# A gated recurrence on one core: one transpose of 128 columns in place of two of 64, and another division of the input products over the steps

## The chip, the cores and the metric

The kernel runs on one core of one Trainium2 chip. The core has a matrix engine (TensorE, PE in the profile; its weight loads are the row PEld), a vector engine (VectorE, DVE), a scalar engine (ScalarE, ACT), a general engine (GpSimd, POOL) and a queue that issues most of the DMAs (SyncE, SP). TensorE writes its results into PSUM, from where VectorE and ScalarE read them; all other data is in SBUF. The metric is the device time of one execution in microseconds (us), and a smaller one is better.

## The reference

The input `x` has 8 sequences of 512 steps with 512 features, and `cond_1024` is the first state `h`, 8 by 512. The result is `x` plus the states of this recurrence:

```
fused = sigmoid(concat([x_t, h]) @ w_W + w_b)
r, z = split(fused)
m = x_t @ wx_W + wx_b + r * (h @ wh_W + wh_b)
h = z * h + (1 - z) * tanh(m)
```

All is in float32. The 512 steps depend on each other through `h`. The products with `x_t` don't.

## The kernel before

**Layout.** The 512 units of the state are cut into four quarters of 128 (index `k` as input, `c` as output) with 32 units of each quarter in each quarter of the partitions. Two output quarters are called half A, the other two half B. The state of each half and step is a tile `hTA` or `hTB`, in eight buffers (L150). The batch is only 8, so one matrix multiplication holds four steps' columns as 32 stationary columns, of which a step uses eight rows of the result. The four parts `j` of the result (32 rows each) are computed by four matrix multiplications side by side on the array (L388). A float32 multiplication is recorded as two MATMUL rows, so that one `k` of a product is eight MATMUL rows, in two groups of four that run together.

**One step.** The steps run in the order of the program (L366); each engine takes its instructions in the order in which they are written. TensorE's order is the constant `ORDER` (L27): bank A (256 columns for the two `k` of hTA, then 192 for the two of hTB), bank D (128 columns for each of the four `k`), bank H (64 columns, two `k`), and then one portion of products with `x` for later steps, which the generator `products` (L296) hands out up to its next `yield` (L393). Bank A holds the three raw values of half A (h, z and r, 64 columns each) and 64 columns that half B needs; bank D holds half B's z and r; bank H the rest of half B's h. There are two sets of banks, one for four steps, then the other.

After the matrix work VectorE and ScalarE make the next state. For half A: `turn_r(0)`, `turn_h(0)`, `turn_z(0)` (L470 to L472), each a VectorE transpose of 64 columns out of bank A; ScalarE takes the sigmoid of r into `md0A` and of minus z into `hd0A`; two scans `memory(0, 0)` and `memory(0, 1)` on VectorE (L462) form the argument of tanh; ScalarE writes tanh into the state tile (L463). For half B: `turn_part` (L452) out of bank A, `turn_r(1)` (L477) out of bank D, `turn_h(1)` (L479) out of bank H, `turn_z(1)` (L480) out of bank D. Between them stand the two scans `update(0, 0)` and `update(0, 1)` (L465) that make the next hTA. Then come `memory(1, 0)`, `memory(1, 1)`, the tanh of half B, and `update(1, 0)`, `update(1, 1)`, that make the next hTB. The next step's bank A needs hTA for its first two `k` and hTB for its last two. `update(0, 1)` is made to wait for half B's sigmoid of r (`r_done`, L481), and `memory(1, 0)`, that reads its result, comes behind it. The tiny memsets of the tile `idle` (L441 behind `turn_z(0)`, and two at the end of each step, L570) are places for waits and delays: L441 waits for the transpose of `turn_h(0)`.

**The input products.** Two groups of four steps share one set of products (six products of half size and a shared one, with sums `sx` made on GpSimd by `x_sum` and weight differences `tw`). They are made during eight steps. Each portion is two groups of four parts per set of columns, from a generator with eight `yield`s: 384 columns in each of four steps, then 288, 96 and 192, 192 and 96, and 288, which is 288 in each of four. The first portion falls on the step with i mod 8 = 4. The generator runs for 62 sets, steps 4 to 499; steps 500 to 511 have no product. The sums and copies that the products need are made at the end of certain steps (L507 to L561); among them `x_sum(o + 2, 2)` at u = 3, where u is i mod 8.

Of the kernel before, what the change touches and what calls it, by code (L numbers as in the profile page):

```python
# [7 lines left out]
F32 = mybir.dt.float32  # L8
BF16 = mybir.dt.bfloat16
AF = mybir.ActivationFunctionType  # L10
# [3 lines left out]
P = 128  # L14
# [3 lines left out]
HU = 64  # L18
# [1 line left out]


DVE_FILL = 23
IDLE = 3
LAST = 4
SYNC = mybir.DependencyInfo(mybir.DependencyClass.Sync, mybir.DependencyReason.DATA)

# [22 lines left out]
def tile_cond_rnn_residual(  # L49
# [39 lines left out]
    nc = tc.nc  # L89
# [7 lines left out]
    work = ctx.enter_context(tc.tile_pool(name="work", bufs=4))  # L97
# [54 lines left out]
    md0 = [[pair(n, f"md0{n}{i}", 32, m) for i in range(2)] for n, m in (("A", 2), ("B", 3))]  # L152
# [72 lines left out]
    def act(key, out_, in_, func, **kw):  # L225
        inst = nc.scalar.activation(out_, in_, func, **kw).ins  # L226
# [58 lines left out]
    def x_sum(o, n):  # L285

        t_ = [q[o % 2] for q in sx]
        a, b, op = [
            (x_half(o, 1, 0), x_half(o, 1, 1), ALU.add),
            (t_[0], x_half(o, 0, 0), ALU.subtract),  # L290
            (x_half(o, 0, 0), x_half(o, 1, 0), ALU.subtract),
            (x_half(o, 0, 1), t_[1], ALU.subtract),
        ][n]
        nc.gpsimd.tensor_tensor(t_[n], a, b, op)

    def products(o):  # L296

        t_ = [q[o % 2] for q in sx]
        p1 = (0, x_half(o, 0, 0), wx_of(0, 0))
        p2 = (0, x_half(o, 0, 1), wx_of(1, 0))  # L300
        p3 = (0, t_[3], wx_of(1, 1))
        p4 = (1, x_half(o, 1, 1), tw[3])
        p6 = (0, t_[1], tw[1])
        p7 = (1, t_[2], tw[2])

        def pair(left, right, k, c0=0, c1=WIDE):
            for j in range(NQ):
                bank, lhs, rhs = left if j < 2 else right
                mm(
                    xps[bank][32 * j : 32 * j + 32, COLS.start + c0 : COLS.start + c1],  # L310
                    lhs[:, k],
                    rhs[:, k, j % 2, c0:c1],
                    start=right is p7 and k == 0 and j >= 2,
                )
# [10 lines left out]
        pair(p1, p7, 0)  # L325
        yield
        pair(p1, p7, 1)
        yield
        pair(p2, p6, 0)
        yield  # L330
        pair(p2, p6, 1)
        yield
        pair(p4, p3, 0, 0, 288)
        yield
        pair(p4, p3, 0, 288)
        shared(0)
        yield
        shared(1)
        pair(p4, p3, 1, 0, 96)
        yield  # L340
        pair(p4, p3, 1, 96)
        yield

    def take(it, n=None):
        while n is None or n > 0:
# [20 lines left out]
    for i in range(T):  # L366
        g, s = divmod(i, GS)
        c, t = divmod(i, TC)
        ps = banks[g % 2]
# [5 lines left out]
        for n in (ORDER if i else FIRST).split():  # L375
# [3 lines left out]
            bank, k = n[0], int(n[1])  # L379
# [15 lines left out]
        rows = slice(B * s, B * s + B)  # L395

        def scan(c_, out_, d0, d1):
# [6 lines left out]
            ).ins  # L404

        pa = ps["A"][:, HU:] if i else xps[0][:, :HALF]
        raw = {
            "h": (pa[:, :HU], ps["H"]),
            "z": (pa[:, HU : 2 * HU], ps["D"][:, :HU]),
            "r": (pa[:, 2 * HU :], ps["D"][:, HU:]),  # L410
        }

        def turned(n, hf):
            t_ = work.tile([P, 2, 32], F32, tag=f"t{n}{hf}", name=f"t{n}{hf}_{i}")
            inst = nc.vector.transpose(t_.rearrange("p c n -> p (c n)"), raw[n][hf]).ins  # L415
            return t_[:, :, rows], inst

        r_done = [None, None]
        h_done = [None, None]

        def turn_r(hf):
            tr, _ = turned("r", hf)
            r_done[hf] = act(
                ("r", hf, g % 2, s),
                md0[hf][g % 2][:, rows, :, 1 + hf].rearrange("p n c -> p c n"),
                tr,
                AF.Sigmoid,
            )
# [9 lines left out]
        def turn_z(hf):  # L438
            tz, _ = turned("z", hf)
            if hf == 0:  # L440
                inst = nc.vector.memset(idle[:, IDLE - 1 :], 0.0).ins  # L441
                tc.add_manual_dep(inst, h_done[0].name, SYNC)
            act(
                ("zc", hf, i % 2),
                hd0[hf][i % 2][:, :, :, 2].rearrange("p n c -> p c n"),
                tz,
                AF.Sigmoid,
                scale=-1.0,
            )

        def turn_part():
            nc.vector.transpose(md1[1][g % 2][:, :, :, 0].rearrange("p n c -> p c n"), ps["A"][:, :HU])  # L452
# [18 lines left out]
        turn_h(0)  # L471
        turn_z(0)  # L472
        memory(0, 0)
        memory(0, 1)
        if i:
            turn_part()
        turn_r(1)  # L477
        update(0, 0)
        turn_h(1)  # L479
        turn_z(1)  # L480
        tc.add_manual_dep(update(0, 1), r_done[1].name, SYNC)  # L481
        if i == 0:
# [9 lines left out]
        memory(1, 0)  # L492
        memory(1, 1)
        update(1, 0)
        update(1, 1)
# [5 lines left out]
        o, u = divmod(i, 2 * GS)  # L501
        nxt, two = o + 1 < NG // 2, o + 2 < NG // 2
# [15 lines left out]
        if u == 0:  # L518
            spread(2 * o + 1, "D")
            if o and nxt:  # L520
                nc.scalar.copy(xps[0][Q01, lo], step_bias[Q01])
                nc.scalar.copy(xps[1][Q23, lo], step_bias[Q23])
        elif u == 1:
            spread(2 * o + 1, "A")
            if o == 0:
                seed(3)
        elif u == 2:
            if o == 0:
                nc.scalar.copy(xs[0][:, SC], xps[0][:, COLS])
            elif nxt:  # L530
                nc.scalar.copy(both[Q23, HALF:], xps[0][Q01, lo])
                nc.vector.tensor_copy(both[Q23, :HALF], xps[1][Q23, lo])
            if two:
                nc.scalar.copy(xps[0][Q01, COLS], bias[Q01, COLS])
        elif u == 3:
            if o == 0:
                nc.scalar.copy(xs[1][:, SC], xps[1][:, COLS])
            if two:
                x_sum(o + 2, 2)
        elif u == 4 and nxt:  # L540
            if o:
                add_(xs[1][Q01, SC], xps[1][Q01, COLS], u3[Q23], ALU.add)
            spread(2 * o + 2, "A")
            if two:
                x_sum(o + 2, 0)
        elif u == 5 and nxt:
            if o:
                add_(xs[1][Q23, SC], u3[Q23], both[Q23], ALU.add)
            if two:
                nc.scalar.copy(xps[0][Q23, COLS], xps[0][Q01, COLS])  # L550
                x_sum(o + 2, 1)
            spread(2 * o + 2, "D")
        elif u == 6 and nxt:
            spread(2 * o + 2, "H")
            if two:
                nc.vector.memset(xps[1][Q01, COLS], 0.0)
# [12 lines left out]
        for n in range(IDLE - 1):  # L569
# [101 lines left out]
```

## Time and profile before

| | |
|---|---|
| three timed runs | 1681.18, 1681.23, 1681.54 us; median 1681.23 us |
| profiled execution | 1681.52 us, of which 1679.7 us are its span, from the first instruction to the last |
| granted TensorE clock | 1.000 |
| busy in the span | VectorE 1402.8 us, ScalarE 1190.5 us, GpSimd 327.2 us; for TensorE see below |
| DMA | 30.14 MB; the DMA engines are busy under a tenth of the time after the first of 40 slices |

A row of the timeline view has the start in us from the span's start, the time from the first start to the last end, engine, line and operation, what is written and read with shapes, and how many instructions were merged (x16). In brackets stands the idle time of that engine in front of it and what ended it. A row of the groups view has count, busy time in us, mean ns of one, and the idle time of the engine in front of them. A matrix multiplication's row is longer than the time until the next one may start, so spacing is read from start to start. A VectorE row likewise overlaps the next by some 0.05 to 0.10 us, and where the instruction waits, part of the wait can stand within it.

### The profile page before, as it was taken

How to read it: one execution, taken by the hardware profiler on the slowest of the kernel's cores; microseconds unless marked ns; L12 is line 12 of the kernel's file. 1: busy time of each engine (PE TensorE's matmuls, PEld its weight loads, DVE VectorE, ACT ScalarE, POOL GpSimd, SP SyncE). 2: the span in 40 equal slices, each digit the busy share in tenths (PEclk: the TensorE clock that was granted, in tenths of full speed). 3: DMA queues.
4: the chain of work that ended last, by engine and by line, in shares of the span. 5: the costliest groups of instructions: out<-in, count | busy, mean ns of one | idle time of the engine just before them, and what ended most of it. 6: DMA issues, size and time to landing. Idle time of an engine off the chain costs nothing.

```text
span 1679.7 us, 110201 instructions
## 1 busy us (share of the span) xinstructions
PE 1667.8 (99%) x46078; PEld 1237.3 (74%) x46078; DVE 1402.8 (84%) x10213; ACT 1190.5 (71%) x5884; POOL 327.2 (19%) x1290
## 2 busy tenths in 40 slices
PE   8999999999999999999999999999999999999998
PEld 5777777777777777777777777777777777777776
DVE  6888888888888888888888888888888888888886
ACT  4777777777777777777777777777777777777775
POOL 2221121111211211112112121121121211211211
PEclk9999999999999999999999999999999999999999
DMA  4000000000000000000000000000000000000000
GB/s 178 17 4 17 17 17 17 12 9 17 17 17 17 4 17 17 17 17 4 17 17 17 17 16 5 17 17 17 17 4 17 17 17 17 4 17 11 11 11 10
DMA packets 11452, 30.14 MB, mean 18 GB/s; under 512 B 1220, under 2 KB 1732, under 8 KB 10952
## 3 DMA queue, kind: packets, MB, share of 16 engines
q1 hardware_dynamic: 10800, 22.94, 3.9%
q8 instruction: 360, 5.90, 1.5%
q14 instruction: 140, 1.15, 0.2%
q10 hardware_dynamic: 152, 0.16, 0.0%
HBM read 14.70 MB, written 8.39 MB: 14 GB/s over the span
## 4 chain that ended last, share of the span: by engine, by line
PE 97%; DVE 2%; DMA 1%; ACT 0%; issue 0%
PE A L195 48%; PE D L195 26%; PE xp L195 17%; PE H L195 7%; DMA wd<-in_wd_dram 1%; DVE tr L415 0%; DMA rows<-in_bias_dram 0%; DVE m L399 0%; DVE md1B L452 0%; DVE tw L283 0%; DVE tz L415 0%; DVE md1A L431 0%; DVE hTA L399 0%; DVE hTB L399 0%; ACT hTB L226 0%
## 5 line engine op out<-in xcount | busy, mean ns | idle before, releaser
L195 PE MATMUL A<-wa,hTA 128*32 128x256 f32 x8176 | 535.3, 379 | 3.0 <-DVE hTA L399 3.0
L195 PE MATMUL A<-wa,hTB 128*32 128x192 f32 x8176 | 436.2, 331 | 0.0
L195 PEld LDWEIGHTS A<-wa,hTA 128*32 128x32 f32 x8176 | 255.6, 122 | 233.0 <-DVE hTA L399 171.3
L572 POOL TENSOR_TENSOR ot<-xin,hTB 128x16 f32<-128x16 f32 x503 | 124.8, 248 | 1312.0 <-DVE hTB L399 1301.0
L195 PEld LDWEIGHTS A<-wa,hTB 128*32 128x32 f32 x8176 | 250.8, 123 | 165.8 <-DVE hTB L399 145.4
L195 PE MATMUL D<-wd,hTA 128*32 128x128 f32 x8192 | 317.6, 273 | 1.2 <-DMA wd<-in_wd_dram 1.2
L195 PE MATMUL D<-wd,hTB 128*32 128x128 f32 x8192 | 317.5, 273 | 0.0
L226 ACT ACTIVATE md0A<-tr 128x16 f32<-128x16 f32 x512 | 112.8, 220 | 231.0 <-DVE tr L415 221.6
L195 PEld LDWEIGHTS D<-wd,hTA 128*32 128x32 f32 x8192 | 257.2, 122 | 22.2 <-DMA wd<-in_wd_dram 1.5
L195 PE MATMUL xp<-tw,sx 128*32 128x384 f32 x1984 | 265.3, 406 | 0.0
L415 DVE STREAM_TRANSPOSE tr<-A 128x64 f32<-128x64 f32 x511 | 127.9, 250 | 137.0 <-PE A L195 127.7
L195 PEld LDWEIGHTS D<-wd,hTB 128*32 128x32 f32 x8192 | 240.4, 122 | 0.0
L399 DVE TENSOR_TENSOR_SCAN hTB<-hd0B,hTB 128x24 f32<-128x24 f32 x1024 | 159.9, 198 | 94.4 <-ACT hTB L226 94.4
L195 PE MATMUL H<-wa,hTB 128*32 128x64 f32 x8192 | 208.2, 219 | 0.0
L195 PE MATMUL xp<-wx,xin 128*32 128x384 f32 x1056 | 207.9, 486 | 0.0
L399 DVE TENSOR_TENSOR_SCAN hTA<-hd0A,hTA 128x24 f32<-128x24 f32 x1024 | 194.8, 190 | 0.0
L195 PEld LDWEIGHTS H<-wa,hTB 128*32 128x32 f32 x8192 | 185.5, 122 | 0.0
L226 ACT ACTIVATE hTB<-hTB 128x16 f32<-128x16 f32 x512 | 121.3, 237 | 78.4 <-DVE hTB L399 66.2
L226 ACT ACTIVATE hd0B<-tz 128x16 f32<-128x16 f32 x512 | 115.7, 226 | 74.9 <-DVE tz L415 27.6
L226 ACT ACTIVATE hTB<-m 128x8 f32<-128x8 f32 x1024 | 163.8, 208 | 4.4
L226 ACT ACTIVATE hTA<-m 128x8 f32<-128x8 f32 x1024 | 160.5, 206 | 2.2
L399 DVE TENSOR_TENSOR_SCAN m<-md0A,md1A 128x16 f32<-128x16 f32 x1024 | 142.2, 181 | 8.8
(103 smaller groups left out, 2586.2 us busy)
## 6 DMA issues: line engine op xcount, KB each, us to landing
xin<-in_x_dram SPq DMA_DIRECT2D x31, 256.0 KB, 3.5
out_dram<-ot SPq DMA_DIRECT2D x31, 256.0 KB, 2.1
wx<-in_wx_dram SPq DMA_DIRECT2D x4, 768.0 KB, 6.8
wa<-in_wa_dram SPq DMA_DIRECT2D x4, 512.0 KB, 9.6
wd<-in_wd_dram SPq DMA_DIRECT2D x1, 768.0 KB
wd<-in_wd_dram SPq DMA_DIRECT2D x1, 256.0 KB, 11.2
out_dram<-ot SPq DMA_DIRECT2D x1, 192.0 KB, 1.9
head<-in_xh_dram ACTq DMA_DIRECT2D x1, 144.0 KB, 4.8
```

What stands on the lines that cost most here:

```text
L195: nc.tensor.matmul(out_, lhsT, rhs, start=start, stop=False, skip_group_check=True)
L226: inst = nc.scalar.activation(out_, in_, func, **kw).ins
L399: return nc.vector.tensor_tensor_scan(*[t_[:, :, c_].rearrange("p n c s -> p (n c s)") for t_ in (out_, d0, d1)], 0.0, ALU.mult, ALU.add,).ins
L415: inst = nc.vector.transpose(t_.rearrange("p c n -> p (c n)"), raw[n][hf]).ins
L572: return engine.tensor_tensor(ot[:, t, 2 * hf : 2 * hf + 2, :].rearrange("p c n -> p n c"), x_of(c, slice(2 * hf, 2 * hf + 2), t, 1).rearr ...
```

## The change

Two things are changed together.

First, half B's two transposes out of bank D become one of all 128 columns, `turn_rz`, at the place of `turn_r(1)`. Behind it ScalarE takes both sigmoids, r first. `turn_z(1)` is gone from its place between `turn_h(1)` and `update(0, 1)`. `update(0, 1)` no longer waits for the sigmoid of r; `memory(1, 0)` itself does. A new memset `settle(1)` of `idle` behind `update(0, 1)` waits for the transpose of `turn_h(1)`, so that `memory(1, 0)` has only one wait of its own. `memory(1, 0)` is written a few lines earlier, which changes the order only in the last step.

Second, the products are divided anew: each set's first 128 columns of its first product (k = 0) go into the step before, with the last 192 columns of the set before it. The portions are 384 in two of eight steps and 320 in six (the very first portion has 448 columns, the very last 192). Three more pieces per set are needed: 13 in place of 10. `x_sum(o + 2, 2)` is made one step earlier, since its first reader is.

```
+        pair(p1, p7, 0, 0, 128)
+        if o > 2:
+            yield
+        pair(p1, p7, 0, 128)
+        pair(p1, p7, 1, 0, 64)
         yield
-        pair(p1, p7, 1)
+        pair(p1, p7, 1, 64)
         yield
         pair(p2, p6, 0)
         yield
         pair(p2, p6, 1)
         yield
-        pair(p4, p3, 0, 0, 288)
+        pair(p4, p3, 0, 0, 320)
         yield
-        pair(p4, p3, 0, 288)
+        pair(p4, p3, 0, 320)
         shared(0)
+        pair(p4, p3, 1, 0, 64)
         yield
         shared(1)
-        pair(p4, p3, 1, 0, 96)
+        pair(p4, p3, 1, 64, 192)
         yield
-        pair(p4, p3, 1, 96)
-        yield
+        pair(p4, p3, 1, 192)
...
+        def settle(hf):
+            inst = nc.vector.memset(idle[:, IDLE - 2 + hf : IDLE - 1 + hf], 0.0).ins
+            tc.add_manual_dep(inst, h_done[hf].name, SYNC)
...
+        def turn_rz():
+            t_ = work.tile([P, 4, 32], F32, tag="trz", name=f"trz_{i}")
+            nc.vector.transpose(t_.rearrange("p c n -> p (c n)"), ps["D"])
+            act(
+                ("r", 1, g % 2, s),
+                md0[1][g % 2][:, rows, :, 2].rearrange("p n c -> p c n"),
+                t_[:, 2:, rows],
+                AF.Sigmoid,
+            )
+            sigma_z(1, t_[:, :2, rows])
...
-        turn_r(1)
+        turn_rz()
         update(0, 0)
         turn_h(1)
-        turn_z(1)
-        tc.add_manual_dep(update(0, 1), r_done[1].name, SYNC)
+        update(0, 1)
+        settle(1)
...
+        memory(1, 0)
...
                 nc.scalar.copy(xps[0][Q01, COLS], bias[Q01, COLS])
+                if o:
+                    x_sum(o + 2, 2)
         elif u == 3:
             if o == 0:
                 nc.scalar.copy(xs[1][:, SC], xps[1][:, COLS])
-            if two:
                 x_sum(o + 2, 2)
```

The first matrix multiplication of the part that clears its quarter of the bank (`start=`) is now told by `c0 == 0` too, `IDLE` grows from 3 to 4, and `turn_z(0)` is written with the same helpers as before it, `settle(0)` and `sigma_z`; its instructions stay as they were.

More of the change, by code (lines that the diff above doesn't have):

```diff
@@ L22 @@
 DVE_FILL = 23
-IDLE = 3
+IDLE = 4
 LAST = 4
@@ L312, in pair @@
                     rhs[:, k, j % 2, c0:c1],
-                    start=right is p7 and k == 0 and j >= 2,
+                    start=right is p7 and k == 0 and c0 == 0 and j >= 2,
                 )
@@ L323, in shared @@
                 )
-        pair(p1, p7, 0)
+        pair(p1, p7, 0, 0, 128)
[3 more added lines that the diff above has]
+        pair(p1, p7, 1, 0, 64)
         yield
-        pair(p1, p7, 1)
+        pair(p1, p7, 1, 64)
         yield
@@ L406, in tile_cond_rnn_residual @@
         pa = ps["A"][:, HU:] if i else xps[0][:, :HALF]
[L407 to L411, printed above, removed]
+        raw = {"h": (pa[:, :HU], ps["H"]), "z": (pa[:, HU : 2 * HU],), "r": (pa[:, 2 * HU :],)}
         def turned(n, hf):
@@ L416, in turned @@
             return t_[:, :, rows], inst
-        r_done = [None, None]
         h_done = [None, None]
@@ L422, in turn_r @@
             tr, _ = turned("r", hf)
-            r_done[hf] = act(
+            act(
                 ("r", hf, g % 2, s),
@@ L436, in turn_h, with sigma_z @@
                 tc.add_manual_dep(inst, pool_done[i + 1 - NH].name, SYNC)
[L438 to L442, printed above, removed]
+        def sigma_z(hf, tz):
             act(
@@ L449, in turn_z @@
             )
+        def settle(hf):
+            inst = nc.vector.memset(idle[:, IDLE - 2 + hf : IDLE - 1 + hf], 0.0).ins
+            tc.add_manual_dep(inst, h_done[hf].name, SYNC)
+        def turn_z(hf):
+            tz, _ = turned("z", hf)
+            settle(hf)
+            sigma_z(hf, tz)
+        def turn_rz():
+            t_ = work.tile([P, 4, 32], F32, tag="trz", name=f"trz_{i}")
+            nc.vector.transpose(t_.rearrange("p c n -> p (c n)"), ps["D"])
+            act(
+                ("r", 1, g % 2, s),
[4 more added lines that the diff above has]
+            sigma_z(1, t_[:, :2, rows])
         def turn_part():
@@ L491, in tile_cond_rnn_residual @@
             )
-        memory(1, 0)
         memory(1, 1)
@@ L568, in tile_cond_rnn_residual @@
                 nc.vector.tensor_tensor(step_bias[to], bias[Q23, c_], bias[Q01, c_], ALU.subtract)
-        for n in range(IDLE - 1):
+        for n in range(IDLE - 2):
             nc.vector.memset(idle[:, n : n + 1], 0.0)
```

## Prediction

> **What bounds the kernel now.** I read the page first, then TensorE's timeline of one block of eight steps in the middle, then the same of the last steps.
>
> ```profile
> span 1679.7 us, 110201 instructions
> PE 1667.8 (99%) x46078; PEld 1237.3 (74%) x46078; DVE 1402.8 (84%) x10213; ACT 1190.5 (71%) x5884; POOL 327.2 (19%) x1290
> ...
> PE 97%; DVE 2%; DMA 1%; ACT 0%; issue 0%
> ...
> L195 PEld LDWEIGHTS A<-wa,hTB 128*32 128x32 f32 x8176 | 250.8, 123 | 165.8 <-DVE hTB L399 145.4
> ```
>
> By these TensorE is everything. But a matmul's row lasts longer than the matmul holds the array, so 99% can hide waits, and the weight loads of hTB do wait for VectorE. The spacing of starts decides:
>
> ```profile
> 796.96 1.05 PE L195 MATMUL A<-wa,hTA 128*32 128x256 f32 x16
> ...
> 800.05 1.05 PE L195 MATMUL A<-wa,hTA 128*32 128x256 f32 x16
> ...
> 803.26 1.05 PE L195 MATMUL A<-wa,hTA 128*32 128x256 f32 x16
> 804.19 0.87 PE L195 MATMUL A<-wa,hTB 128*32 128x192 f32 x16
> ...
> 809.68 1.05 PE L195 MATMUL A<-wa,hTA 128*32 128x256 f32 x16
> ...
> 812.73 0.49 PE L195 MATMUL xp<-wx,xin 128*32 128x384 f32 x2
> ...
> 813.05 1.05 PE L195 MATMUL A<-wa,hTA 128*32 128x256 f32 x16
> 813.91 0.83 PE L195 MATMUL A<-wa,hTB 128*32 128x192 f32 x16
> ...
> 822.81 1.05 PE L195 MATMUL A<-wa,hTA 128*32 128x256 f32 x16
> ```
>
> The block is 796.96 to 822.81, 25.85 us. The steps that start at 796.96 to 806.47 carry 288 product columns, the four from 809.68 carry 384. From 813.05 on three steps take 9.76, so 3.253 each, and there hTB's matmuls begin 0.86 after hTA's (813.91). Where the step before had 288 columns they begin 0.93 after (804.19). TensorE waits there for hTB, and the first weights of hTB load late. A group of 384 columns takes 0.32 (812.73 to 813.05), so a portion of two groups loses 2 x 96 x 0.32/384 = 0.16 when 96 columns go. A step with 288 columns could take 3.09, which 796.96 to 800.05 shows. The next takes 3.21 (800.05 to 803.26), and the wait that the last of the four causes falls into the next step (809.68 to 813.05, 3.37 = 3.25 + 0.12). So each of the four costs 3.21. The last steps, which have no products, show what that is:
>
> ```profile
> 1650.12 1.08 PE L195 MATMUL A<-wa,hTA 128*32 128x256 f32 x16 [0.24 <-DVE hTA L399]
> ...
> 1669.39 1.09 PE L195 MATMUL A<-wa,hTA 128*32 128x256 f32 x16 [0.24 <-DVE hTA L399]
> ```
>
> Six steps in 19.27 are 3.21 each, with nothing for TensorE to fill in. 3.21 is the loop from bank A through VectorE and ScalarE to hTB and back into bank A, and no portion under about 358 columns (384 less 0.043/0.107 x 64) makes a step shorter than that. A block is 4 x 3.253 + 4 x 3.21 = 25.85.
>
> **The change, part by part.** Portions first. 320 columns take 2 x 64 x 0.32/384 = 0.107 off 3.253, so 3.146 as far as TensorE goes, below 3.21. If the loop stays as it is, two steps move from 3.253 to 3.21 and nothing else happens. So the loop decides. This is its second half, half B's, in a step with 288 columns, with half A's scans ahead:
>
> ```profile
> 802.21 0.22 ACT L226 ACTIVATE md0A<-tr 128x16 f32<-128x16 f32 x1 [0.15 <-DVE tr L415]
> ...
> 802.47 0.28 DVE L399 TENSOR_TENSOR_SCAN m<-md0A,md1A 128x16 f32<-128x16 f32 x2
> ...
> 802.55 0.41 PE L195 MATMUL H<-wa,hTB 128*32 128x64 f32 x16
> ...
> 802.77 0.25 PE L195 MATMUL xp<-tw,xin 128*32 128x96 f32 x2
> ...
> 802.81 0.24 DVE L415 STREAM_TRANSPOSE tr<-D 128x64 f32<-128x64 f32 x1
> ...
> 802.97 0.17 DVE L399 TENSOR_TENSOR_SCAN hTA<-hd0A,hTA 128x24 f32<-128x24 f32 x1
> 803.06 0.25 DVE L431 STREAM_TRANSPOSE md1B<-H 128x64 f32<-128x64 f32 x1
> 803.09 0.22 ACT L226 ACTIVATE md0B<-tr 128x16 f32<-128x16 f32 x1
> 803.20 0.21 PEld L195 LDWEIGHTS A<-wa,hTA 128*32 128x32 f32 x8
> 803.21 0.21 DVE L415 STREAM_TRANSPOSE tz<-D 128x64 f32<-128x64 f32 x1
> ...
> 803.34 0.21 DVE L399 TENSOR_TENSOR_SCAN hTA<-hd0A,hTA 128x24 f32<-128x24 f32 x1
> ...
> 803.47 0.28 DVE L399 TENSOR_TENSOR_SCAN m<-md0B,md1B 128x24 f32<-128x24 f32 x2
> ...
> 803.93 0.31 DVE L399 TENSOR_TENSOR_SCAN hTB<-hd0B,hTB 128x24 f32<-128x24 f32 x2 [0.18 <-ACT hTB L226]
> ```
>
> The path: transpose of r (ends 803.05), sigmoid (803.09 to 803.31), then `update(0, 1)`, which was told to wait for that sigmoid and also stands behind the transpose of z (803.34), then half B's scans (803.47), tanh, hTB. Two things change on it.
>
> It gains: the scans wait for the sigmoid themselves. Before, they start 0.16 after its end (803.47 - 803.31). Half A's scans, which wait directly, start 0.04 after (802.47 - 802.43). The difference is 0.12. A VectorE row can hold part of its wait (hTA's scan lasts 0.17 at 802.97 and 0.21 at 803.34, where it waits), so the direct start may be some 0.02 later than recorded, and I take 0.10.
>
> It loses: the sigmoid waits for 128 columns. No row shows such a transpose; call its extra time p. Bounds:
>
> ```profile
> L532 DVE COPY both<-xp 64x192 f32<-64x192 f32 x62 | 22.4, 361 | 1.9
> ...
> L210 DVE COPY bias<-xp 128x512 f32<-128x512 f32 x1 | 0.7, 692 | 1.0 <-PE xp L195 1.0
> ...
> L265 DVE STREAM_TRANSPOSE md1A<-xp 128x32 f32<-128x32 f32 x2 | 0.3, 196 | 2.2 <-ACT A L260 2.2
> ...
> L431 DVE STREAM_TRANSPOSE md1A<-xp 128x64 f32<-128x64 f32 x1 | 0.2, 208 | 0.0
> ```
>
> From below, transposes of 32 and 64 columns out of PSUM differ by 12 ns, so 64 more cost 24. From above, a whole second transpose, 0.13 (803.21 to 803.34, start to next start). Between them, VectorE copies out of PSUM rise by 331 ns for 320 columns, which is 66 ns for 64. I take 0.066, because there the price per column is measured over many columns, while the two transposes differ by less than their fixed part varies.
>
> So hTB comes 0.10 - 0.066 = 0.034 sooner after bank A, and the loop is 3.21 - 0.034 = 3.176. It stays over 3.146, so TensorE still waits a little.
>
> The added memset is the second condition for the scans. It waits for the transpose out of bank H (803.06 to 803.31). That one starts later now, pushed by p: 803.12, end 803.37. The row at 803.21 that used to stand behind it is gone, `update(0, 1)` starts by 803.27, the memset after both, by about 803.41 to 803.46, and the scans are ready for the sigmoid at 803.38 + 0.04 = 803.42. So it is nearly level, where the transpose takes 0.25. In steps whose portions read `wx` and `xin` with 384 columns it takes longer:
>
> ```profile
> 815.98 0.30 DVE L431 STREAM_TRANSPOSE md1B<-H 128x64 f32<-128x64 f32 x1
> ```
>
> With 0.05 more the memset is the later one by about as much as the path gained. Two of the six steps with 320 columns (i mod 8 = 4 and 5) have these products, so I leave them at 3.21, and take 3.176 for the other four. Behind the memset stand only half B's scans, hTB's scans and the step's closing work on VectorE. TensorE waits for them, and that is the loop.
>
> What is hidden: hTA's first scan moves from 802.97 to about 803.04, pushed by p, and ends at 803.21 in place of 803.14. Its weights were loaded 0.06 after that end (803.20), so now at 803.27. The products cover it: they ended at 803.26 with 288 columns and end 2 x 32 x 0.32/384 = 0.05 later with 320, at 803.31. That leaves 0.04, and once it is used up, each 0.01 costs 0.01 per step. The transpose of z was 0.13 of VectorE in front of `update(0, 1)`; with it gone, what is late next is the sigmoid. ScalarE's sigmoid of z follows r's at once and ends by about 803.6 (803.38 and one of 0.22), and hTB starts at 803.93. `x_sum` moves a step earlier on GpSimd, whose queue holds the two small sums of the output behind it. GpSimd is busy for 19%, and the bank A transpose waits for those sums only seven steps later. No DMA and no instruction on SP's queue moves. Three more pieces per block on TensorE: four groups of 64 columns took 0.22 (802.55 to 802.77), 0.055 each against 64 x 0.32/384 = 0.053, so a piece costs some 2 ns per group, under 0.02 per block, in steps where TensorE waits anyway: nothing.
>
> By the Trainium skill (TensorEngine Tiling (Array Packing), Instruction Overhead) each matmul has an overhead of about 60 cycles, and small pieces would then not be free. Three pieces of two groups at 25 ns are 0.15 per block by that page, an estimate, or 9 us over the run if nothing hid it. The 0.055 per 64-column group above does not show it.
>
> The sum, per block: 2 x 3.253 + 4 x 3.176 + 2 x 3.21 = 25.63, against 25.85: 0.22 less. 62 blocks give 13.6. The 12 steps without products gain 0.034 each, 0.4. The profiled execution took 1681.52 us, 1.8 of them outside its span, which stay. 1681.52 - 14.0 = 1667.5; the median of the runs, 1681.23, is 0.3 lower. Forecast **1667.2 us**.
>
> **The rivals.**
> 1. *The loop falls under TensorE's own time.* With p at its lower bound the path gains 0.076, the memset does not bind, and all six steps take 3.15: 6.51 + 18.9 = 25.41, 0.44 less per block, 27.3 in all, with the last steps some 28: 1653. If p is 0.066 and the memset binds nowhere, 6.51 + 6 x 3.176 = 25.56 gives 1663. For it: the slow bank H transposes may go with the width of 384. Against: nothing shows a transpose at 24 ns per 64 columns beyond two single rows.
> 2. *The gain on the path is lost to the memset in every step.* Then hTB comes when it came, and only the portions count: 6.51 + 6 x 3.21 = 25.77, 0.08 less per block, 5 in all: 1676. For it: the estimate above has the memset's end and the sigmoid's nearly level.
> 3. *Slower: the wide transpose is two transposes in one, p = 0.13.* Then the sigmoid and everything behind it come 0.03 later than before, the six steps take 3.24, the block 25.95, 0.10 more, and the run 1687.6. It decides from p = 0.114 on, where six steps at 3.224 make up a block of 25.85. For it: the transpose before shows no rate per column of its own. Against: copies out of PSUM pay 1.03 ns per column, half of that.
>
> ```profile
> L195 PEld LDWEIGHTS xp<-tw,xin 128*32 128x32 f32 x992 | 47.0, 110 | 4.0
> ```
>
> 4. *The added pieces show on TensorE.* If each of the three exposed a weight load (0.11 by the row above is the bound), three steps would take 3.146 + 0.11 = 3.26, 0.2 more per block than the forecast, and the run 1680. The 64-column row speaks against it.
>
>
> **How the numbers follow.** Forecast and its neighbourhood (1663 to 1672): 0.45. Rival 1 (1653 to 1663): 0.22. Rival 2 (1672 to 1678): 0.13. Between rivals 2 and 3, or rival 4 (1678 to 1684.6): 0.07. Rival 3: 0.13. Faster by over 0.2% (3.4 us, about what a measurement of this kernel can tell from no change) is the sum of the first three, 0.80; within 0.2%, 0.07; slower, 0.13. The range from 1653 to 1680 leaves out rival 3 and some of the case before it.
>
> **What would show it.** In the profile after: the wide transpose's row lasts about 0.28 to 0.31 where tr lasted 0.24, which is p. Half B's scans start 0.04 after the sigmoid of r ends, or later if the memset holds them. Bank A's starts are 3.18 apart in four steps of a block, 3.21 in two, 3.25 in two; in the last steps, 3.18. If they are 3.15 in all six, rival 1 holds; if the last steps still take 3.21, rival 2; over 3.22, rival 3. The sum fails if a chain that I hold for hidden (hTA's first scan, above all) ends last once hTB's is shorter.

## The result, and the profile after

The changed kernel takes 1665.71 us (median of four runs, 1665.45 to 1666.54), the kernel before 1681.38 us beside it (1681.18 to 1681.67). The ratio is 0.9907, with a 95% interval from 0.989 to 0.9925, so the change is faster by 15.7 us. The forecast was 1667.2 us, in a range from 1653 to 1680.

From the page of the kernel after (its span, the busy times, the chain that ended last by engine, and two groups of weight loads):

```profile
span 1664.0 us, 113147 instructions
PE 1650.5 (99%) x47566; PEld 1272.1 (76%) x47566; DVE 1391.8 (84%) x10213; ACT 1132.3 (68%) x5884; POOL 327.4 (20%) x1290
...
PE 97%; DVE 2%; DMA 1%; issue 0%; ACT 0%; DVEq 0%
...
L195 PEld LDWEIGHTS A<-wa,hTA 128*32 128x32 f32 x8176 | 258.5, 122 | 175.9 <-DVE hTA L403 94.1
...
L195 PEld LDWEIGHTS A<-wa,hTB 128*32 128x32 f32 x8176 | 244.0, 124 | 154.8 <-DVE hTB L403 135.1
```

hTA's loads before:

```profile
L195 PEld LDWEIGHTS A<-wa,hTA 128*32 128x32 f32 x8176 | 255.6, 122 | 233.0 <-DVE hTA L399 171.3
```

The page looks as it did: TensorE 99% busy, nearly alone on the chain. The weight loads wait less for VectorE: hTB's 135.1 us where it was 145.4, and hTA's 94.1 where it was 171.3. How much of either TensorE feels can't be read from them, since the loads of hTA overlap the products. For that one has to look inside a step. VectorE's timeline of one block of eight steps (start, duration, instruction):

```profile
797.80 0.25 DVE L415 STREAM_TRANSPOSE tr<-A 128x64 f32<-128x64 f32 x1 [0.77 <-PE A L195]
...
801.86 0.31 DVE L457 STREAM_TRANSPOSE trz<-D 128x128 f32<-128x128 f32 x1
...
802.18 0.25 DVE L430 STREAM_TRANSPOSE md1B<-H 128x64 f32<-128x64 f32 x1
802.32 0.17 DVE L403 TENSOR_TENSOR_SCAN hTA<-hd0A,hTA 128x24 f32<-128x24 f32 x1
802.47 0.20 DVE L403 TENSOR_TENSOR_SCAN m<-md0B,md1B 128x24 f32<-128x24 f32 x1
802.49 0.06 DVE L447 MEMSET idle<- 128x1 f32 x1
...
804.16 0.25 DVE L415 STREAM_TRANSPOSE tr<-A 128x64 f32<-128x64 f32 x1
...
805.36 0.26 DVE L430 STREAM_TRANSPOSE md1B<-H 128x64 f32<-128x64 f32 x1
...
807.35 0.25 DVE L415 STREAM_TRANSPOSE tr<-A 128x64 f32<-128x64 f32 x1 [0.19 <-PE A L195]
...
810.53 0.25 DVE L415 STREAM_TRANSPOSE tr<-A 128x64 f32<-128x64 f32 x1
...
813.79 0.25 DVE L415 STREAM_TRANSPOSE tr<-A 128x64 f32<-128x64 f32 x1 [0.29 <-PE A L195]
...
814.99 0.31 DVE L430 STREAM_TRANSPOSE md1B<-H 128x64 f32<-128x64 f32 x1
...
815.34 0.20 DVE L403 TENSOR_TENSOR_SCAN m<-md0B,md1B 128x24 f32<-128x24 f32 x1
...
817.04 0.25 DVE L415 STREAM_TRANSPOSE tr<-A 128x64 f32<-128x64 f32 x1 [0.32 <-PE A L195]
...
823.40 0.25 DVE L415 STREAM_TRANSPOSE tr<-A 128x64 f32<-128x64 f32 x1 [0.77 <-PE A L195]
```

The transposes `tr` out of bank A mark the steps. Eight steps take 823.40 - 797.80 = 25.60 us, where they took 25.85. The two with 384 product columns are those from 810.53 and 813.79, 3.26 and 3.25. The other six take (25.60 - 6.51)/6 = 3.18. The wide transpose lasts 0.31, half B's transpose of r lasted 0.24 before.

ScalarE's sigmoid of r in the same two steps, from its timeline:

```profile
802.20 0.23 ACT L226 ACTIVATE md0B<-trz 128x16 f32<-128x16 f32 x1
...
815.01 0.23 ACT L226 ACTIVATE md0B<-trz 128x16 f32<-128x16 f32 x1
```

These two steps tell the conditions of half B's first scan apart. At 802.43 the sigmoid and bank H's transpose (802.18 + 0.25) end together, and the scan starts 0.04 later. In the later step the sigmoid ends at 815.24, the transpose, 0.31 long, at 815.30, and the scan starts at 815.34: 0.10 after the sigmoid, 0.04 after the transpose. So what it follows is the transpose, through the memset; where the transpose is short, the sigmoid is level with it. The whole trace agrees: on the mean of each of the eight places in a block the scan starts 0.04 after the transpose's end, but from 0.04 to 0.10 after the sigmoid's. (The memset's row starts after the scan's although it stands ahead of it in the order: the start of a waiting row is not to be trusted to 0.02.)

The last steps, without products, in TensorE's timeline:

```profile
1641.13 1.09 PE L195 MATMUL A<-wa,hTA 128*32 128x256 f32 x16 [0.30 <-DVE hTA L403]
...
1657.00 1.09 PE L195 MATMUL A<-wa,hTA 128*32 128x256 f32 x16 [0.30 <-DVE hTA L403]
```

Five steps in 15.87 are 3.174 each, where they were 3.21.

### The profile page after: what moved, and what is told of

Same layout as the page of the kernel before. It is cut to its first block, busy times and chain, and to the rows that moved or that the text cites. A ratio compares the mean times of both kernels' runs of the same rounds, so it can differ in the third digit from the quotient of the medians.

```text
span 1664.0 us, 113147 instructions
## 1 busy us (share of the span) xinstructions
PE 1650.5 (99%) x47566; PEld 1272.1 (76%) x47566; DVE 1391.8 (84%) x10213; ACT 1132.3 (68%) x5884; POOL 327.4 (20%) x1290
## 4 chain that ended last, share of the span: by engine, by line
PE 97%; DVE 2%; DMA 1%; issue 0%; ACT 0%; DVEq 0%
PE A L195 47%; PE D L195 26%; PE xp L195 17%; PE H L195 7%; DMA wd<-in_wd_dram 1%; DVE m L403 0%; DMA rows<-in_bias_dram 0%; DVE tr L415 0%; DVE trz L457 0%; DVE md1B L467 0%; DVE tw L283 0%; DVE md1A L430 0%; DVE tz L415 0%; DVE hTA L403 0%; DVE hTB L403 0%
## 5 line engine op out<-in xcount | busy, mean ns | idle before, releaser
L195 PEld LDWEIGHTS A<-wa,hTA 128*32 128x32 f32 x8176 | 258.5, 122 | 175.9 <-DVE hTA L403 94.1
L195 PEld LDWEIGHTS A<-wa,hTB 128*32 128x32 f32 x8176 | 244.0, 124 | 154.8 <-DVE hTB L403 135.1
L195 PE MATMUL xp<-tw,sx 128*32 128x192 f32 (+5 forms) x2480 | 276.3, 358 | 0.0
L195 PE MATMUL xp<-wx,xin 128*32 128x384 f32 (+4 forms) x1552 | 218.9, 384 | 0.0
L403 DVE TENSOR_TENSOR_SCAN hTA<-hd0A,hTA 128x24 f32<-128x24 f32 x1024 | 171.0, 167 | 0.0
L226 ACT ACTIVATE md0B<-trz 128x16 f32<-128x16 f32 x512 | 116.4, 227 | 73.5 <-DVE trz L457 12.0
L403 DVE TENSOR_TENSOR_SCAN m<-md0B,md1B 128x24 f32<-128x24 f32 x1024 | 154.4, 192 | 3.4
```

The source lines that it names most:

```text
L195: nc.tensor.matmul(out_, lhsT, rhs, start=start, stop=False, skip_group_check=True)
L403: return nc.vector.tensor_tensor_scan(*[t_[:, :, c_].rearrange("p n c s -> p (n c s)") for t_ in (out_, d0, d1)], 0.0, ALU.mult, ALU.add,).ins
```

## The experiments

Each kernel was timed in turn with the kernel before on the same chip; "before" is the median of those runs.

| kernel | us | before | ratio (95% interval) |
|---|---|---|---|
| the change | 1665.71 | 1681.38 | 0.9907 (0.989 to 0.9925) |
| e1 portions alone | 1676.63 | 1681.62 | 0.9971 (0.996 to 0.9982) |
| e2 transposes and waits alone | 1672.81 | 1681.62 | 0.9948 (0.9935 to 0.996) |
| e3 two transposes side by side | 1696.46 | 1681.84 | 1.0087 (1.0073 to 1.0101) |
| e4 z at its old place | 1673.19 | 1681.62 | 0.9951 (0.9938 to 0.9963) |
| e5 scan first | 1670.12 | 1681.62 | 0.9931 (0.9919 to 0.9943) |
| e6 no memset | 1701.90 | 1681.84 | 1.0119 (1.0105 to 1.0133) |
| e7 e4 with bank H's transpose split | 1726.00 | 1681.84 | 1.0265 (1.0251 to 1.0279) |
| e8 the change, split likewise | 1721.86 | 1681.84 | 1.0238 (1.0225 to 1.0252) |
| e9 without bank H's transpose | 1663.36 | 1680.90 | 0.9896 (0.9879 to 0.9912) |
| e10 without z | 1655.41 | 1680.90 | 0.9848 (0.9834 to 0.9863) |
| e11 waits exchanged | 1666.96 | 1680.90 | 0.9917 (0.9902 to 0.9932) |
| e12 336 columns in all steps | 1661.10 | 1680.90 | 0.9881 (0.9867 to 0.9896) |

The theory: the loop through half B's first scan sets every step that TensorE doesn't, and the change takes 0.034 us off it; TensorE's own time is met only in the steps with 384 columns. The rivals: one of the two parts brings everything; or the gain comes from something other than the scan's two conditions.

### The two parts, each alone (e1, e2)

e1 has the change's lines in `products` and for `x_sum`, and the old `turn_r(1)`, `turn_z(1)` and waits. e2 is the reverse: the new transposes and waits, and the old portions.

```
 # e1, beside the changed kernel
-        turn_rz()
+        turn_r(1)
         update(0, 0)
         turn_h(1)
-        update(0, 1)
-        settle(1)
+        turn_z(1)
+        tc.add_manual_dep(update(0, 1), r_done[1].name, SYNC)
 # e2, beside the changed kernel
-        pair(p1, p7, 0, 0, 128)
-        if o > 2:
-            yield
-        pair(p1, p7, 0, 128)
-        pair(p1, p7, 1, 0, 64)
+        pair(p1, p7, 0)
         yield
...
```

> The transposes of before (two of 64 columns, update(0,1) waiting for half B's sigmoid of r), with the new division of the products (320 columns in six steps, 384 in two) and x_sum at its new place. Theory (the loop over VectorE, ScalarE and TensorE holds 3.21 us in every step with 320 columns, and only the two steps with 384 columns are TensorE's): 2 x 3.253 + 6 x 3.21 = 25.77 us per block of eight, 0.09 less than before, x 62 blocks = 5.3: about 1676 us. Rival A (the division alone brings it all, the transpose nothing): 1666 us. Rival B (only the transposes count): 1681 us.

> The wide transpose and the new order of half B's operations, with the products divided as before (384 columns in four steps, 288 in four). Theory: the four steps with 288 columns go from 3.21 to 3.18 us, the four with 384 stay TensorE's at 3.253: 0.03 x 4 x 62 = 7.7 us and 0.4 in the last steps: about 1673 us. Rival A (the transpose pays only with the new division): 1681 us. Rival B (the transposes bring it all): 1666 us.

Measured: 1676.63 and 1672.81, 5.0 and 8.8 us less than before. Both are the theory's own numbers, and both rivals of each fall. The portions alone move two steps of a block from TensorE's 3.253 to the loop's 3.21 and stop there. The new transposes and waits alone shorten the four steps with 288 columns. Together they give 15.7, 1.9 more than 5.0 + 8.8. More was to be expected, since the two steps that the portions free fall to a loop that is shorter too; but 0.034 in each of them would be 4.2, so this accounts for the sign and not for the size.

### What in the new transposes gains: z at its old place, and both side by side (e4, e3)

```
 # e4, beside the changed kernel
-        turn_rz()
+        turn_r(1)
         update(0, 0)
         turn_h(1)
+        turn_z(1)
         update(0, 1)
         settle(1)
 # e3, beside the changed kernel
-        turn_rz()
+        turn_r(1)
+        turn_z(1)
         update(0, 0)
         turn_h(1)
```

> The new division and the new order of waits (update(0,1) without a wait, half B's first scan waiting for the sigmoid of r itself, the small memset holding the wait for bank H's transpose), but with two transposes of 64 columns: r at the wide one's place, z after turn_h(1) as before. Theory (the gain of the loop comes from the direct wait, and the wide transpose is a loss of 0.066 us that its saved transpose has to pay back): the scan comes after tr(D), hTA's first addition, bank H's transpose, tz(D), update(0,1) and the memset, some 1.50 us after the step's start against 1.515 in the changed kernel: steps of 3.17 to 3.18 us, 1661 to 1666 us. Rival (the gain needs the wide transpose, since the second transpose stands ahead of the scan again): steps of 3.21, 1676 us.

> The changed kernel with two transposes of 64 columns, r then z, side by side in the place of the wide one; all else as it is, the order of the waits too. Half B's sigmoid of r is then ready some 0.066 us earlier, and bank H's transpose, which stands behind both on VectorE, comes later by what two transposes take more than the wide one. Theory (in the changed kernel the end of bank H's transpose, through the memset, lets half B's first scan go, not the sigmoid): the second transpose puts it and the scan back by about 0.06 to 0.07 us: six steps of about 3.24, two of 3.255: 25.95 per block, 1687 us, slower than before. Rival (the sigmoid of r decides): six steps at or under 3.15, 1654 us.

e4 came out at 1673.19, between theory and rival and nearer to the rival. Its VectorE timeline shows why, with ScalarE's sigmoid of r behind it:

```profile
802.51 0.24 DVE L430 STREAM_TRANSPOSE md1B<-H 128x64 f32<-128x64 f32 x1
802.65 0.21 DVE L415 STREAM_TRANSPOSE tz<-D 128x64 f32<-128x64 f32 x1
802.78 0.17 DVE L403 TENSOR_TENSOR_SCAN hTA<-hd0A,hTA 128x24 f32<-128x24 f32 x1
802.88 0.20 DVE L403 TENSOR_TENSOR_SCAN m<-md0B,md1B 128x24 f32<-128x24 f32 x1
...
802.53 0.22 ACT L226 ACTIVATE md0B<-tr 128x16 f32<-128x16 f32 x1
```

Bank H's transpose and the sigmoid both end at 802.75, but half B's scan starts only at 802.88: from 802.65 on each instruction follows the one before it (0.13, then 0.10), with no wait among them. Freed of the roundabout wait, the scan is held by VectorE's queue, with z's transpose in it. So the direct wait brings only 3.4 us (1676.63 to 1673.19), and the rest, 7.5 us, needs z's transpose out of that place, for which the wide one pays 0.066. Only the two together bring the 0.034. (The reverse of e4, the wide transpose with `update(0, 1)` still waiting for the sigmoid, was not run.) My theory for e4, that the wide transpose is nothing but a loss, is wrong.

e3 was slower than before, on the theory's side: the sigmoid is early there, bank H's transpose is late, and the kernel follows the transpose. In VectorE's timeline of a step with 384 columns the scan starts 0.04 after the transpose's end (804.07), and 0.22 after that of the sigmoid (803.89 in ScalarE's timeline):

```profile
803.77 0.30 DVE L430 STREAM_TRANSPOSE md1B<-H 128x64 f32<-128x64 f32 x1
...
804.11 0.20 DVE L403 TENSOR_TENSOR_SCAN m<-md0B,md1B 128x24 f32<-128x24 f32 x1
```

The 1696 is more than the 1687 that I expected, since I had left the two steps with 384 columns at TensorE's 3.255. There bank H's transpose lasts 0.30, and their loop takes 3.30 too. The other six steps are 3.25 on the mean of the trace where I had 3.24.

### The two conditions of the scan: memset, sigmoid, transpose (e6, e9, e11)

```
 # e6, beside the changed kernel
-        settle(1)
 # e9, beside the changed kernel
-        turn_h(1)
+        if i < 2 * GS:
+            turn_h(1)
         update(0, 1)
-        settle(1)
+        if i < 2 * GS:
+            settle(1)
 # e11, beside the changed kernel: the memset waits for the sigmoid
-            act(
+            h_done[1] = act(
                 ("r", 1, g % 2, s),
...
-            h_done[hf] = inst
+            if hf == 0:
+                h_done[hf] = inst
```

> The changed kernel without the memset of half B: the first scan carries both waits, that for bank H's transpose and that for the sigmoid of r. Theory (the memset adds a link of its own between the transpose and the scan): the scan's end, 0.245 us behind the transpose's end now, moves to where the sigmoid lets it go, 5 to 25 ns earlier: 0.005 to 0.025 x 6 x 62 = 2 to 9 us less, 1657 to 1664 us. Rival A (the wait for the transpose's end costs the same whoever carries it): 1665.7 us, no change. Rival B (a scan with two waits costs more than a memset with one): slower, about 1670 us for 10 ns a step.

> The changed kernel without half B's transpose out of bank H and without the memset that waits for it, from the ninth step on: that part of half B's sums stays at an old value, the rest of the work is done. Theory (in the changed kernel the sigmoid of r and bank H's transpose with its memset let half B's first scan go at nearly the same moment, the scan ending 0.241 us after the one and 0.245 after the other): with the transpose gone the sigmoid still holds the scan, and only the two steps in which the transpose took 0.26 gain: six steps of 3.175 to 3.18, 1663 to 1665 us. Rival (bank H's transpose alone holds the loop): TensorE's own 3.146 in six steps, 1653 us.

> The changed kernel with the two waits exchanged: the memset of half B waits for the sigmoid of r, the first scan itself for bank H's transpose. Theory (without the memset the scan ended 0.312 us behind bank H's transpose instead of 0.245, because one scan with two waits pays about 0.066 for the second): with one wait each it makes no difference who carries which, the scan's end moves by 4 ns at most: 1664 to 1667 us. Rival (what costs is that the scan waits for VectorE's own transpose itself): about 0.066 more per step, as without the memset: 1700 us.

e6 takes 1701.9, 36.2 more than the changed kernel. I had expected a gain, so that theory fell, and of the rivals B has the direction, at seven times its size. VectorE's timeline of e6, with ScalarE's sigmoid of r behind it:

```profile
808.43 0.25 DVE L430 STREAM_TRANSPOSE md1B<-H 128x64 f32<-128x64 f32 x1
...
808.78 0.31 DVE L403 TENSOR_TENSOR_SCAN m<-md0B,md1B 128x24 f32<-128x24 f32 x2
...
808.46 0.23 ACT L226 ACTIVATE md0B<-trz 128x16 f32<-128x16 f32 x1 [0.15 <-DVE trz L457]
```

The scan starts 0.10 after the end of bank H's transpose (808.68 to 808.78) in place of 0.04; the sigmoid, at 808.69, ends level with the transpose. The loss, 36.2 us over 512 steps, is 0.07 a step. The first two lines of its page tell what came in:

```profile
span 1699.2 us, 113145 instructions
...
PE 1685.1 (99%) x47566; PEld 1267.5 (75%) x47566; DVE 1399.5 (82%) x9701; ACT 1131.7 (67%) x5884; POOL 326.8 (19%) x1290
```

VectorE's count falls by the 512 memsets (10213 to 9701), yet all instructions together fall only by 2 (113147 to 113145), with the other engines' counts as they were. So 510 instructions of a kind that isn't counted as busy came in, about one per step. By the Trainium skill (Perfetto Trace Analysis, Identifying Dependency Chains) an instruction that waits for several engines may get EventSemaphore instructions in front of it; the counts here agree. The traces name them: VectorE has 12 records of EVENT_SEMAPHORE in the changed kernel and 522 in e6. e11 confirms that it is the second wait and not the kind of wait: with the two exchanged, one on each instruction, it takes 1666.96 (ratio 0.9917 against 0.9907 for the change, intervals overlapping).

e9 leaves the transpose and the memset out and gains little, as the theory had it: some 2 us by the ratios (0.9896 against 0.9907, the intervals overlap), 3.6 beside e11, which ran with it on the same chip. The sigmoid, right behind, takes over. It is not one condition that holds this loop but two that are level.

### How much is left: without z, and the scan first (e10, e5)

```
 # e10, beside the changed kernel
-            nc.vector.transpose(t_.rearrange("p c n -> p (c n)"), ps["D"])
+            nc.vector.transpose(t_.rearrange("p c n -> p (c n)"), ps["D"][:, HU:])
...
 # e5, beside e4
         turn_z(1)
-        update(0, 1)
         settle(1)
...
         memory(1, 0)
+        update(0, 1)
```

> The changed kernel with r alone transposed for half B (64 columns), and z's sigmoid reading r's columns: z is left out. Theory (the 0.066 us that z's columns add to the wide transpose stand ahead of both conditions of half B's first scan, the sigmoid and bank H's transpose): the scan comes 0.06 earlier, more than the 0.035 that TensorE waits per step, and six steps fall to TensorE's own 3.146: 25.39 per block, 1652 to 1654 us, which is the bound of any better place for z. Rival (another chain, hTA's, is just below the loop): steps stay at 3.16 or more, 1658 us or more.

> As the kernel with z's transpose after turn_h(1), but with the memset and half B's first scan ahead of update(0,1). Theory (half B's first scan starts the loop's last stretch, and is held by whatever stands ahead of it on VectorE once its sigmoid is there): it can start as soon as the sigmoid of r and bank H's transpose allow, some 0.06 us earlier than in the changed kernel, and the loop falls below TensorE's own 3.146 us in the steps with 320 columns: about 2 x 3.253 + 6 x 3.15 = 25.41 per block, 1654 us. Rival (update(0,1) gives hTA's second half, on which bank A's weight loads wait, and it is now late by one scan, 0.18 us or more): steps of 3.25 us or longer, 1690 us or more.

e10 takes 1655.41, near its forecast. In TensorE's timeline a block is 798.17 to 823.64, 25.47. The first two steps take 3.15 each, the next, the first with 384 columns, 3.30:

```profile
798.17 1.05 PE L195 MATMUL A<-wa,hTA 128*32 128x256 f32 x16
...
804.47 1.05 PE L195 MATMUL A<-wa,hTA 128*32 128x256 f32 x16
...
807.77 1.05 PE L195 MATMUL A<-wa,hTA 128*32 128x256 f32 x16
...
823.64 1.05 PE L195 MATMUL A<-wa,hTA 128*32 128x256 f32 x16
```

So 0.066 less ahead of both conditions brings the loop down nearly to TensorE's own time, and no other chain of that size lies between. The block is 0.08 over the 25.39 expected; about half of that lies in the one step of 3.30, where 3.255 is TensorE's own. About 10 us (1665.71 to 1655.41) are what any better place for z could still bring with these portions.

e5 tried for that from e4's kernel, got 3.1 us from it (1673.19 to 1670.12), and stayed 4.4 over the changed kernel. The groups of weight loads on its page:

```profile
L195 PEld LDWEIGHTS A<-wa,hTA 128*32 128x32 f32 x8176 | 226.0, 124 | 227.6 <-DVE hTA L403 215.3
...
L195 PEld LDWEIGHTS A<-wa,hTB 128*32 128x32 f32 x8176 | 265.1, 122 | 120.2 <-DVE hTB L403 91.9
```

hTB's loads wait less for VectorE, 91.9 where the changed kernel has 135.1, but hTA's wait 215.3 where it has 94.1: the scan that was put back by the exchange is the one that TensorE needs first. The theory's mechanism is there, the rival's loss too, and little of the gain is left.

### Splitting bank H's transpose (e7, e8)

```
 # e7 beside e4, and e8 beside the changed kernel
-        turn_h(1)
+        turn_half(0)
...
         memory(1, 0)
+        turn_half(1)
         memory(1, 1)
...
+        def turn_half(q):
+            inst = nc.vector.transpose(md1[1][g % 2][:, :, q, 1], ps["H"][:, 32 * q : 32 * q + 32]).ins
+            if q == 0:
+                h_done[1] = inst
```

> The kernel with z's transpose behind bank H's (two transposes of 64 columns), and bank H's transpose of 64 columns divided into two of 32: the first half ahead of half B's first scan, the second between its two scans. Theory (the loop is what stands on VectorE ahead of half B's first scan; in that kernel the scan followed its queue without a gap): about 0.10 us leaves that queue, the first scan ends at about 1.61 us after the step's start and then waits for the sigmoid of r alone, and six steps fall to TensorE's own 3.146: 25.39 per block, about 1653 us, faster than the changed kernel. Rival (the second scan, now behind the second half transpose and its wait, gives the weights that TensorE needs some 0.33 us after the first scan's, and comes up to 0.14 us later than now): six steps of 3.17 to 3.22 us, 1661 to 1680 us.

> The changed kernel with bank H's transpose divided in the same way (32 columns ahead of half B's first scan, 32 between its two scans). Theory (behind bank H's transpose the sigmoid of r, 0.066 us late by the wide transpose, is the next to bind, only 5 to 10 ns below it): 0.10 us taken off the queue gives a gain of 5 to 15 ns in six steps, 2 to 6 us: 1660 to 1664 us. Rival A (the queue alone counts): six steps of 3.146, 1653 us. Rival B (the second scan comes late): 1666 us or more.

Both are far slower, 1726.0 and 1721.86. The rivals had the place right, the second scan; e7's was far too low. VectorE's timeline of e7:

```profile
801.29 0.20 DVE L438 STREAM_TRANSPOSE md1B<-H 128x32 f32<-128x32 f32 x1
801.40 0.21 DVE L415 STREAM_TRANSPOSE tz<-D 128x64 f32<-128x64 f32 x1
...
801.63 0.20 DVE L403 TENSOR_TENSOR_SCAN m<-md0B,md1B 128x24 f32<-128x24 f32 x1
...
801.75 0.20 DVE L438 STREAM_TRANSPOSE md1B<-H 128x32 f32<-128x32 f32 x1
801.98 0.21 DVE L403 TENSOR_TENSOR_SCAN m<-md0B,md1B 128x24 f32<-128x24 f32 x1
```

Half the columns hold VectorE for 0.11 (801.29 to 801.40) in place of e4's 0.14 (802.51 to 802.65), so 0.03 left the queue and not 0.10. I could have known it: 64 columns more cost 0.066, so 32 fewer can save 0.033. And the second scan starts 0.35 after the first, where e4's two scans start 0.12 apart (802.88 and 803.00), because it has to wait for the second transpose to end (801.95). The second half of hTB comes that much later behind the first. How much of these 0.23 each step pays was not worked out; e7 takes some 0.10 a step more than e4 (52.8 us over 512 steps).

### A better division (e12)

e10 and the profile after point at the two steps with 384 columns: they are TensorE's at 3.255 while it waits in the six others. The copy of bank 0 stands between the products of p1 and p7 and those of p2 and p6, so the last had only two portions, 768 columns. Done in column halves, with the copy in two pieces, they can be spread over more.

```
+            pair(p1, p7, 0, 0, HALF)
+            yield
+            pair(p1, p7, 1, 0, HALF)
+            pair(p1, p7, 0, HALF, 336)
+            yield
+            pair(p1, p7, 0, 336)
+            pair(p1, p7, 1, HALF)
+            pair(p2, p6, 0, 0, 96)
+            yield
...
+                x_sum(o + 2, 1)
+                if o:
+                    c_ = slice(COLS.start, COLS.start + HALF)
+                    nc.scalar.copy(xps[0][Q23, c_], xps[0][Q01, c_])
```

> The changed kernel with the products divided into 336 columns in all eight steps in place of 320 in six and 384 in two. For this the products of p1 and p7 go by column halves, bank 0's copy between its halves is made in two pieces a step apart, and the sums of x come a step earlier on GpSimd. Theory (TensorE's own time is now 3.172 everywhere, under the loop of 3.18, so the two steps of 3.255 fall to the loop): 8 x 3.185 = 25.48 per block in place of 25.61: about 1657 us, faster than the changed kernel. Rival (bank H's transpose stays at 0.305 us in the steps that hold the products of wx with xin, and the loop there is 3.24): 6 x 3.185 + 2 x 3.24 = 25.59: about 1664 us, and slower still, 1668 us or more, if the added pieces show.

It takes 1661.10, the best of all kernels with the whole computation: 0.9881 against the change's 0.9907. Beside e11, which is the change but for the exchanged waits and ran on the same chip in the same turn, it is 5.9 us less. In TensorE's timeline a block is 25.56:

```profile
797.38 1.05 PE L195 MATMUL A<-wa,hTA 128*32 128x256 f32 x16
...
822.94 1.05 PE L195 MATMUL A<-wa,hTA 128*32 128x256 f32 x16
```

That is 3.195 a step, between theory and rival. Bank H's transposes in VectorE's timeline tell the rest:

```profile
797.17 0.25 DVE L444 STREAM_TRANSPOSE md1B<-H 128x64 f32<-128x64 f32 x1
800.35 0.30 DVE L444 STREAM_TRANSPOSE md1B<-H 128x64 f32<-128x64 f32 x1
```

They last 0.25 to 0.30, and the loop follows them: the scan starts 0.04 after their end. In the whole trace they last 0.26 to 0.28 on the mean in the five steps of a block whose products read `wx` and `xin`, and 0.25 in the other three. The lengthening moved with the products and did not go away.

## Why the prediction was right, step by step

- **The loop decides, and the portions alone give 1676.** e1 measured 1676.63. Right.
- **The direct wait gains 0.10 and the wide transpose loses 0.066.** The wide transpose lasts 0.31 for 0.24, so p = 0.07. Of the three values that the working had to choose from, the rate of the copies out of PSUM was the right one. The scan starts 0.04 after the sigmoid where both conditions are level, as half A's does. The last steps went from 3.21 to 3.174; the working said 3.176. Right. But the working wrote the 0.10 down to the wait, and named the queue that z's transpose leaves only among what is hidden. e4 shows that with z's transpose still in the queue the wait alone is worth 3.4 us. The one number was right for the whole, not for its parts, and that it came out so closely is partly luck: 0.10 was a measured 0.12 lowered by judgement, and 0.066 was one of three values.
- **The memset is nearly level with the sigmoid.** Right: in the step at 802 both end together, the later step above follows bank H's transpose and not the sigmoid, and e9 gains only some 2 to 4 us by taking it and its memset away. That fits the steps with products, which take 3.18 and not 3.176.
- **Two steps stay at 3.21.** This term was mis-sized. I took 0.30 for bank H's transpose in the two steps whose products read `wx` and `xin`, the length beside 384 columns. In the changed kernel it lasts 0.26 there (805.36, and on the mean of both steps in the trace), beside 320, and these steps take 3.19 and 3.18 (804.16 to 807.35 to 810.53). The 0.05 for two steps and 62 blocks is about 3 us, against some 1 us that the other four fall short; that leaves some 2 us where forecast and result differ by 1.5. VectorE's timeline of e1 has 0.29 in the second of these steps, beside groups of 320 columns too:

```profile
813.58 0.29 DVE L435 STREAM_TRANSPOSE md1B<-H 128x64 f32<-128x64 f32 x1
```

So the width alone doesn't decide, and why this transpose is shorter in the changed kernel stays open.
- **The added pieces cost nothing, and hTA's first scan stays hidden.** TensorE's timeline of the changed kernel, around the start of one step and in the pieces of another:

```profile
808.20 0.44 PE L195 MATMUL xp<-wx,xin 128*32 128x320 f32 x2
...
808.47 0.44 PE L195 MATMUL xp<-wx,xin 128*32 128x320 f32 x2
...
808.73 1.05 PE L195 MATMUL A<-wa,hTA 128*32 128x256 f32 x16
...
821.07 0.23 PE L195 MATMUL xp<-tw,xin 128*32 128x64 f32 x2
...
821.12 0.23 PE L195 MATMUL xp<-tw,xin 128*32 128x64 f32 x2
...
821.18 0.52 PE L195 MATMUL xp<-tw,sx 128*32 128x192 f32 x8
```

Groups of 64 columns follow each other in 0.055 on the mean, the time of their columns. And bank A starts 0.26 after a group of 320 columns, as that group did after the one before it (0.27): hTA's weights were there in time, nothing stands between. Both right.
- **The rivals.** Rival 1 needs the loop under 3.146, and e10 shows that the wide transpose's 0.066 is what keeps it from there. Rival 2 would have left the last steps at 3.21. Rival 3 falls with the row of the wide transpose, p = 0.07 and not 0.13. e3, where two whole transposes stand ahead, is slower than before as well (1.0087), but by another path: there bank H's transpose came late and the sigmoid early. The point of p from which rival 3 decides was not measured. Rival 4 falls with the row of 64 columns.

## What to carry to other kernels

When several things hold an instruction (a wait, a second wait, its engine's queue), work out the time of each: shortening one moves the instruction only to the next, and here two waits were level (scan at 802.47), and the queue would have let it go only some 0.05 earlier (an estimate: 802.32, and the 0.10 from one scan to the next in e4). A second wait on an instruction of the loop can be put on a small one ahead of it on the same engine, which here was worth 0.07 us a step. And once the loop is shorter, look again at the steps that it doesn't set: dividing the products evenly was worth some 5 us more.

## What the runs showed of the hardware that was not expected

- A VectorE scan with two waits starts 0.10 us after the later condition, with one 0.04; with a 0.06 us memset that takes one of the waits it is 0.04 again, whichever wait that is (e11). Over 512 steps the second wait on the scan cost 36 us.
- A VectorE transpose out of PSUM has a large fixed part: 32, 64 and 128 columns last 0.20, 0.21 to 0.25 and 0.31, and one of 32 holds VectorE for 0.11 where one of 64 does for 0.14.
- The transpose out of bank H into a strided tile takes from 0.25 to 0.31 with the same operands: before, after and in e1 and e12 it is longer on the mean only in steps whose products read `wx` and `xin`. In the changed kernel it is longest beside groups of 384 columns, but e1 has 0.29 beside 320. The cause was not tested and stays open.
